# One pair of batches resident at a time, sums one slot later and deeper rings in a Mamba scan

## The chip, the cores and the metric

The kernel runs on one core of one Trainium2 chip. A core has five engines that work side by side, each through its own instructions in its own order: TensorE (PE, matrix products), VectorE (DVE), ScalarE (ACT, functions such as exp), GpSimd (POOL, slow elementwise work) and SyncE (SP, which here issues all the DMA transfers). SBUF is the memory that the engines work in, PSUM the one that PE writes to [...]. The metric is the device time of one run in microseconds; less is better. Three runs of the kernel before took 9922.25 to 9954.8 us, with a median of 9931.66 us.

## The reference

Four blocks run one after the other on images `x` of 4 batches, 96 channels and 64 x 64 places, read as sequences of L = 4096: a Mamba block with fusion (L0), a second kind of Mamba block over four scan directions (L1), a Mamba block with fusion again (L2), and a ConvNeXt block (L3). The change is in L0 and L2, which are alike:

```python
seq = x.reshape(b, c, L).transpose(0, 2, 1)
for i in range(2):
    seq = seq + _mamba_block(seq, ...)          # below
gp  = relu(x.mean((2, 3)) @ gp_w.T + gp_b)      # from the block's input
out = einsum('oc,bchw->bohw', fus_w, concat([seq as image, gp everywhere])) + fus_b
out = batchnorm(out) + x

# _mamba_block: 192 inner channels d, 16 states s
h = layernorm(seq); xs, z = split(h @ in_w)
xc = silu(conv4(xs) + conv_b)
dt, Bm, Cm = split(xc @ xproj_w)
delta = softplus(dt @ dt_w + dt_b)
dA  = exp(delta[..., None] * A)                 # per place, channel and state
dBx = delta[..., None] * Bm * xc[..., None]
hstates[l] = dA[l] * hstates[l - 1] + dBx[l]    # along the sequence
y = (sum over s of hstates * Cm) + Dp * xc
return (y * silu(z)) @ out_w
```

All numbers are 32-bit floats. The state along the sequence is what makes this expensive: 192 channels x 16 states per batch and place.

## The kernel before

The four stages follow each other in `program`: `mamba_fusion`, `ssd`, `mamba_fusion`, `convnext`. Only `mamba_fusion` changes, which runs twice.

**How its work is cut.** Batches go in pairs, and sequences in 8 chunks of T = 512. A step is (pair, layer `sub`, chunk): 2 x 2 x 8 = 32 steps a stage. The 2 x 192 inner channels of a pair fill three tiles of 128 partitions, numbered j. Inside a step the 16 states and 8 channels at a time make the 128 partitions of a scan. A group (GS = 2) is two such scans, so a step has 24 groups: j (3) x q (4) x half (2). A stage has 32 x 24 = 768 groups.

**One group** goes through these methods of `Scan`:

- `load`: DMA of the step sizes delta from a DRAM copy, each row spread over 16 partitions, into a tile `da` of 128 x 1024. For every fourth group (`dma`) a second tile `du` of the same ring is loaded, with delta times xc. The ring has 6 tiles.
- `spread`: PE makes `bs`, delta times xc spread over states, by a matmul with a selection matrix (L313), into one of two PSUM tiles of two banks. For a `dma` group, ACT writes the exponentials there instead, and POOL multiplies `du` by B (L308).
- `decay`: ACT makes the exponentials dA in place in `da` (L107).
- `scan`: DVE multiplies `bs` by B (L335; not in a `dma` group), then scans twice (L340) into `hs`; POOL multiplies `hs` by C into `hc` (L342); ACT keeps the last column in `carry` (L345). `hs` and `hc` are rings of 3.
- `sums`: PE adds the 16 states of `hc` into a PSUM tile `py` (L361), one per j and step; the term Dp * xc is a matmul into the same tile (L355).
- `close`, after the last group of a j: DVE multiplies `py` by silu(z) (L369). `project`: PE applies out_w (L377), DVE adds the result to `X` (L381). `fuse`, in the second layer alone: PE applies fus_w, ACT adds the bias, DVE takes statistics, and SyncE stores to DRAM (L507 to L513).

**What sets the order.** `Scan.run` walks over slots n. In slot n it calls `close` for group n-3, then `load` for n+4, `spread` for n+1, `decay` for n+2, `scan` for n and `sums` for n-2, then `project` for n-4 and `fuse` for n-5, and at last one or two pieces of `mamba_front` of the next step (`PACE`), so that layer norm, the input products (`pu`, `pz`), xproj (`pd`), softplus (`pt`, `delta`, `lg`) and the stores of delta are spread over the step. The framework that builds the program puts in the semaphores, gives a ring's tile again only when all that used it have finished, and may shift an instruction against the others on its engine; on the chip each engine takes its instructions in the resulting order. A wait at the head of an engine's queue so holds all that is behind it there.

**X.** `X` holds the sequence of all four batches in SBUF (96 x 4 x 4096) for the whole stage. It is loaded at the stage's start, layer 0 updates it, layer 1 updates it again, and `fuse` replaces each chunk by the fused output. During the first front DVE takes the sum of each batch (L532, `gsum`) for the global branch `gp`.

Of the kernel before, what the change touches and what calls it, by code (L numbers as in the profile page):

```python
# [18 lines left out]
F32 = mybir.dt.float32  # L19
AF = mybir.ActivationFunctionType  # L20
ALU = mybir.AluOpType
AX = mybir.AxisListType
# [132 lines left out]
def mamba_front(tc, k, X, pools, wt, pair, c, h, made):  # L155
# [14 lines left out]
    for b in range(2):  # L170
        pc = bank("pc")[:C]
        nc.tensor.matmul(
            pc, lhsT=k.center, rhs=X[:, 2 * pair + b, ds(c * T, T)], start=True, stop=True
        )
        sq = work.tile([P, T], F32, tag="ua", name="sq")[:C]
        nc.scalar.activation(sq, pc, AF.Square)
        yield
        pv = bank("pv")[:C]
        nc.tensor.matmul(pv, lhsT=k.mean, rhs=sq, start=True, stop=True)
        rs = work.tile([P, T], F32, tag="lg", name="rs")[:C]  # L180
        rsqrt(k.act, rs, pv, k.eps[:C])
        yield
        dst = h[:C, b, 3 : 3 + T]
        nc.vector.tensor_tensor(dst, pc, rs, ALU.mult)
        nc.gpsimd.tensor_scalar(dst, dst, wt["ln"][:, 0:1], wt["ln"][:, 1:2], ALU.mult, ALU.add)
# [88 lines left out]
class Scan:  # L274
# [13 lines left out]
    def load(self, g):  # L288

        for name, which in (("da", "dd"), ("du", "dg")) if g["dma"] else (("da", "dd"),):  # L290
            g[name] = self.state.tile([P, GS, T], F32, tag="da", name=name, bufs=6)
            for i in range(GS):
                r = QUART * g["quarters"][i] + HEIGHT * g["q"]
                src = g["made"][which, g["j"]][r : r + HEIGHT].partition_broadcast(NST)
                self.tc.nc.sync.dma_start(g[name][:, i], src)
# [34 lines left out]
    def scan(self, g):  # L330
        nc = self.tc.nc
        c, j = g["c"], g["j"]
        da, dbx = g["terms"]
        if not g["dma"]:
            nc.vector.tensor_tensor(dbx, dbx, self.b_or_c(g, 0), ALU.mult)  # L335
        hs = self.state.tile([P, GS, T], F32, name="hs", bufs=3)
        for i in range(GS):
            n = NQU * g["quarters"][i] + g["q"]
            init = 0.0 if c == 0 else self.carry[:, j, n : n + 1]
            nc.vector.tensor_tensor_scan(hs[:, i], da[:, i], dbx[:, i], init, ALU.mult, ALU.add)  # L340
        g["hc"] = self.state.tile([P, GS, T], F32, name="hc", bufs=3)
        nc.gpsimd.tensor_tensor(g["hc"], hs, self.b_or_c(g, 1), ALU.mult)  # L342
        if c < NT - 1:
            n = NQU * g["quarters"][0] + g["q"]
            nc.scalar.copy(self.carry[:, j, n : n + 2 * NQU + 1 : 2 * NQU], hs[:, :, T - 1])  # L345
# [25 lines left out]
    def project(self, g, b):  # L371

        nc = self.tc.nc
        xz, wt = g["made"]["xz"], g["wt"]
        po = self.psum.tile([P, T], F32, tag="po", name="po", bufs=1)[:C]
        for n, (j, r0, r1) in enumerate(ROWS[b]):
            nc.tensor.matmul(  # L377
                po, lhsT=wt["out"][r0:r1, j], rhs=xz[r0:r1, j], start=(n == 0), stop=(n == 1)
            )
        xs = self.X[:, 2 * g["pair"] + b, ds(g["c"] * T, T)]  # L380
        nc.vector.tensor_tensor(xs, xs, po, ALU.add)  # L381

    def run(self, steps, wts, front, first):
# [10 lines left out]
        ]  # L394
        total, each = len(groups), len(units)
        ahead = iter(())
        for n in range(-4, total + 6):
            slot = (n + LEAD) % each
            if slot == 0:
                for _ in ahead:  # L400
# [4 lines left out]
            def at(lag):  # L405
                return groups[n - lag] if 0 <= n - lag < total else None

            if (g := at(3)) and g["last"]:
                self.close(g)
            for stage, lag in (  # L410
                (self.load, -4), (self.spread, -1), (self.decay, -2), (self.scan, 0), (self.sums, 2),
            ):
                if g := at(lag):
                    stage(g)

            for lag, what in ((4, self.project), (5, self.fuse)):
                if (g := at(lag)) and g["last"] and g["j"] and (g["sub"] or lag == 4):
                    what(g, g["j"] - 1)
            for _ in range(PACE[slot] if slot < len(PACE) else 0):
                next(ahead, None)  # L420
# [46 lines left out]
def mamba_fusion(ctx: ExitStack, tc, k, src, dst, w):  # L467

    nc = tc.nc
    one = ctx.enter_context(tc.tile_pool(name="m1", bufs=1))  # L470
    X = one.tile([C, B, L], F32, name="X")
    for b in range(2):
        nc.sync.dma_start(X[:, b, :T], src[b, :, :T])
    work = ctx.enter_context(tc.tile_pool(name="mwork", bufs=1))
# [29 lines left out]
    stats = one.tile([C, B * NT, nc.vector.BN_STATS_DIM], F32, name="stats")  # L504

    def fuse(g, b):
        b, c = 2 * g["pair"] + b, g["c"]  # L507
        xs = X[:, b, ds(c * T, T)]
        pf = psum.tile([P, T], F32, tag="po", name="pf", bufs=1)[:C]
        nc.tensor.matmul(pf, lhsT=fus[:, 0], rhs=xs, start=True, stop=True)  # L510
        nc.scalar.activation(xs, pf, AF.Identity, bias=gb[:, b : b + 1])
        nc.vector.bn_stats(stats[:, b * NT + c], xs)
        nc.sync.dma_start(dst[b, :, ds(c * T, T)], xs)  # L513

    wts = [mamba_weights(nc, k.act, k.ident, one, w, 0, one7)]
    carry = one.tile([P, 3, P // HEIGHT], F32, name="carry")
# [3 lines left out]
        pair, sub, c = steps[n]  # L520
        return mamba_front(tc, k, X, (work, psum, dram), wts[sub], pair, c, h, made)

    for b in range(B):
        rest = slice(T if b < 2 else 0, L)
        nc.sync.dma_start(X[:, b, rest], src[b, :, rest])

    gsum = one.tile([C, B], F32, name="gsum")
    made = {}
    for n, _ in enumerate(front(0, made)):
        if n % 4 == 3 and n // 4 - 1 in range(B):  # L530
            b = n // 4 - 1
            nc.vector.reduce_sum(gsum[:, b : b + 1], X[:, b], axis=AX.X)  # L532
    wts.append(mamba_weights(nc, k.act, k.ident, one, w, 1, one7))

    gpw = one.tile([C, C], F32, name="gpw")
# [776 lines left out]
```

## Time and profile before

| stage | about, us | what runs |
|---|---|---|
| first Mamba | 0 to 3,080 | first scan 76.6, last scan ends 3,053 |
| L1 | 3,100 to 6,190 | |
| second Mamba | 6,190 to 9,250 | first scan 6,269, last scan ends 9,234 |
| ConvNeXt | 9,250 to 9,939 | |

| engine | busy, us | share of the span |
|---|---|---|
| PE | 8555.7 | 86% |
| DVE | 8200.3 | 83% |
| POOL | 6968.8 | 70% |
| ACT | 5528.2 | 56% |

| group of instructions | times | mean, ns |
|---|---|---|
| L342 POOL hc | 1536 | 2356 |
| L340 DVE scan, with carry, of da | 2016 | 1265 |
| L335 DVE bs times B | 1152 | 1214 |
| L308 POOL du times B | 384 | 2356 |

A group's line in the profile gives line, engine, operation, tiles written and read, shapes, and then busy time, the mean of one, and the idle time of the engine just before them with what ended it. A line of waits reads: engine, tile and line that waited, what it waited for, total us, times and the longest. A line of busy times by stretch gives from:to, length, then busy us and count for PE, PEld (weight loads), DVE, ACT and POOL, then the granted PE clock as a share of full speed, the DMA engines' busy share, and GB/s. A timeline's line gives start, length, engine, line and operation, and in brackets the idle time before it and who ended it. An end of a matmul is modelled, not measured.

### The profile page before, as it was taken

The numbers are of one execution on the slowest core, as the hardware profiler recorded it, in microseconds if no ns is written. First come the engines' busy times: TensorE is split into PE (matmuls) and PEld (weight loads), VectorE is DVE, ScalarE is ACT, GpSimd is POOL, SyncE is SP. The second block draws the span as 40 slices with busy tenths as digits, with TensorE's granted clock in tenths as the row PEclk, the third lists the DMA queues.
The fourth block names the chain that finished last, engine by engine and source line by source line (L and its number), as shares of the span: only waits on it lengthen the run. The fifth ranks groups of instructions, "written<-read, shape, count | busy, mean of one in ns | idle before, by whom it ended". The sixth has DMA issues, their size and how long they took to land. (4 is left out here: it accounts for less than half of the span.)

```text
span 9939.0 us, 109693 instructions
## 1 busy us (share of the span) xinstructions
PE 8555.7 (86%) x32744; PEld 3519.5 (35%) x32744; DVE 8200.3 (83%) x10861; ACT 5528.2 (56%) x10500; POOL 6968.8 (70%) x4600
## 2 busy tenths in 40 slices
PE   7888888888886998998998988788888888888688
PEld 1222212222212676776776776122222222211122
DVE  7999999999995666666666666799999999999787
ACT  5666666566663455555455554566666665665244
POOL 6888888888884555555555555688888888888322
PEclk8999999999997999999999998899999999999798
DMA  7677677677674223222222222767777777776432
GB/s 189 199 204 202 201 207 206 196 205 208 198 206 121 66 71 92 72 69 83 79 74 74 82 67 57 194 199 205 211 204 206 206 203 200 208 203 199 113 97 74
DMA packets 803535, 1528.27 MB, mean 154 GB/s; under 512 B 124253, under 2 KB 128249, under 8 KB 802170
## 3 DMA queue, kind: packets, MB, share of 16 engines
q1 hardware_dynamic: 802938, 1521.25, 54.4%
q8 instruction: 260, 4.26, 0.2%
q14 instruction: 337, 2.76, 0.1%
HBM read 1229.69 MB, written 156.37 MB: 139 GB/s over the span
## 5 line engine op out<-in xcount | busy, mean ns | idle before, releaser
L342 POOL TENSOR_TENSOR hc<-hs,bc 128x1024 f32<-128x1024 f32 x1536 | 3608.0, 2356 | 630.3 <-DVE hs L340 550.9
L340 DVE TENSOR_TENSOR_SCAN hs<-da,carry,bs 128x512 f32<-128x512 f32 x2016 | 2467.0, 1265 | 81.1 <-DVE bs L335 2.7
L107 ACT ACTIVATE da<-da,w_a 128x512 f32<-128x512 f32 x2304 | 1617.2, 716 | 1273.2 <-DMA da<-dd 1229.1
L361 PE MATMUL py<-hc,selsum 128*32 128x512 f32 x6144 | 1797.4, 637 | 469.8 <-POOL hc L342 463.4
L313 PE MATMUL bs<-du,seldu 64*128 64x512 f32 x4608 | 1570.6, 676 | 208.8 <-DVE hs L340 193.0
L335 DVE TENSOR_TENSOR bs<-bs,bc 128x1024 f32<-128x1024 f32 x1152 | 1398.4, 1214 | 180.2 <-PE bs L313 177.3
L308 POOL TENSOR_TENSOR du<-du,bc 128x1024 f32<-128x1024 f32 x384 | 904.7, 2356 | 279.8 <-DMA du<-dg 144.0
L361 PEld LDWEIGHTS py<-hc,selsum 128*32 128x32 f32 x6144 | 239.3, 110 | 1814.3 <-POOL hc L342 1125.4
L879 POOL TENSOR_TENSOR seg<-seg,cb 128x384 f32<-128x384 f32 x512 | 514.8, 1007 | 516.9 <-DVE cb L878 434.0
L863 DVE TENSOR_SCALAR seg<-dr,dac 128x128 f32<-128x128 f32 x1536 | 645.6, 454 | 276.3 <-PE y L908 269.1
L313 PEld LDWEIGHTS bs<-du,seldu 64*128 64x128 f32 x4608 | 445.6, 195 | 1202.6 <-DVE hs L340 857.0
L194 PE MATMUL pu<-h,w_conv 96*128 96x512 f32 (+3 forms) x2048 | 835.3, 628 | 11.7 <-ACT rs L107 11.6
L340 DVE TENSOR_TENSOR_SCAN hs<-bs,carry,du 128x512 f32<-128x512 f32 x672 | 823.6, 1260 | 6.7 <-issue 5.1
L814 PE MATMUL front<-pk,sconv 128*128 128x512 f32 x1536 | 756.7, 610 | 24.5 <-ACT z L802 20.4
L918 POOL TENSOR_TENSOR y<-y,xs 128x192 f32<-128x192 f32 x496 | 294.4, 594 | 626.0 <-DVE y L917 619.7
L931 ACT ACTIVATE y<-yz 128x192 f32<-128x192 f32 x512 | 186.1, 364 | 903.5 <-DVE yz L930 902.5
L883 POOL TENSOR_TENSOR xs<-pre,coef 128x576 f32<-128x576 f32 x512 | 597.1, 1171 | 65.6 <-ACT pre L112 32.4
L825 PE MATMUL front<-sconv,pk 128*128 128x192 f32 x3072 | 572.8, 329 | 51.1 <-DVE pre L830 46.0
L1175 DVE SCALAR_TENSOR_TENSOR acc<-pad,c_conv,acc 96x1024 f32<-96x1024 f32 x336 | 491.8, 1467 | 110.5 <-ACT acc L1166 59.2
L345 ACT COPY carry<-hs 128x2 f32<-128x2 f32 x1344 | 250.7, 187 | 569.7 <-DVE hs L340 566.1
L825 PEld LDWEIGHTS front<-sconv,pk 128*128 128x128 f32 x3072 | 496.5, 190 | 81.8 <-DVE pre L830 72.3
L107 ACT ACTIVATE bs<-da,w_a 128x512 f32<-128x512 f32 x768 | 522.0, 680 | 2.2 <-DMA da<-dd 0.7
(196 smaller groups left out, 13878.7 us busy)
## 6 DMA issues: line engine op xcount, KB each, us to landing
da<-dd SPq DMA_DIRECT2D x3072, 256.0 KB
du<-dg SPq DMA_DIRECT2D x768, 256.0 KB
dr<-rows SPq DMA_DIRECT2D x256, 384.0 KB
bc<-rows SPq DMA_DIRECT2D x256, 256.0 KB
dd<-delta SPq DMA_DIRECT2D x192, 256.0 KB
dg<-du SPq DMA_DIRECT2D x192, 256.0 KB
pk<-xn SPq DMA_DIRECT2D x128, 384.0 KB
pk<-xn SPq DMA_DIRECT2D x128, 256.0 KB
```

The costliest lines, as they stand in the source:

```text
L107: self.last = self.scalar.activation(out, in_, func, **kw)
L194: nc.tensor.matmul(pu[r0:r1], lhsT=wt["conv"][:kk, tap, d0:d1], rhs=h[:kk, b, ds(tap, T)], start=(tap == 0), stop=(tap == 3),)
L308: nc.gpsimd.tensor_tensor(g["du"], g["du"], self.b_or_c(g, 0), ALU.mult)
L313: nc.tensor.matmul(g["bs"][:, i], lhsT=self.sel["du"][rows, g["half"], g["q"]], rhs=g["made"]["du"][rows, g["j"]], start=True, stop=True,)
L335: nc.vector.tensor_tensor(dbx, dbx, self.b_or_c(g, 0), ALU.mult)
L340: nc.vector.tensor_tensor_scan(hs[:, i], da[:, i], dbx[:, i], init, ALU.mult, ALU.add)
L342: nc.gpsimd.tensor_tensor(g["hc"], hs, self.b_or_c(g, 1), ALU.mult)
L361: nc.tensor.matmul(py[rows], lhsT=self.sel["sum"][:, g["q"]], rhs=g["hc"][:, i], start=(g["q"] == 0), stop=(g["q"] == NQU - 1),)
L814: nc.tensor.matmul(p, lhsT=self.conv[:, i, DI + q * DST : DI + (q + 1) * DST], rhs=pk[:, i, ds(c * T, T)], start=(i == 0), stop=(i == 2),)
L825: nc.tensor.matmul(p, lhsT=pk[:, i, ds(c * Q, Q)], rhs=self.conv[:, i, :DI], start=(i == 0), stop=(i == 2),)
L863: nc.vector.tensor_scalar(seg[:, h], g["pair"]["dr"][:, c % 2 * NH + h], made["dac"][:, n0 + h : n0 + h + 1], 0.0, ALU.subtract, ALU.min,)
L883: nc.gpsimd.tensor_tensor(xs, x.to_broadcast([P, 3, NH, HD]), coef.to_broadcast([P, 3, NH, HD]), ALU.mult)
```

## The change

It has three parts.

1. `X` holds one pair of batches (96 x 2 x 4096), half of the SBUF. The second pair's sequences come in chunk by chunk: after `fuse` has stored a chunk of the first pair's output, SyncE loads the second pair's chunk into the same place. The sums for the global branch of batches 2 and 3 are taken ahead from 1024-column pieces that are loaded into tiles of the `da` ring during the first front.
2. `sums` works on group n-3 rather than n-2, and what follows it (`close`, `project`, `fuse`) moves by a slot too.
3. The rings grow with the memory that became free: `da` (step sizes) from 6 to 8 with `load` five slots ahead rather than four, `hs` (states) and `hc` (products) from 3 to 4.

It is meant to give POOL's product a slot more before PE needs it, and the loads more time ahead of their use.

```diff
-            pc, lhsT=k.center, rhs=X[:, 2 * pair + b, ds(c * T, T)], start=True, stop=True
+            pc, lhsT=k.center, rhs=X[:, b, ds(c * T, T)], start=True, stop=True
...
-            g[name] = self.state.tile([P, GS, T], F32, tag="da", name=name, bufs=6)
+            g[name] = self.state.tile([P, GS, T], F32, tag="da", name=name, bufs=8)
...
-        hs = self.state.tile([P, GS, T], F32, name="hs", bufs=3)
+        hs = self.state.tile([P, GS, T], F32, name="hs", bufs=4)
...
-        g["hc"] = self.state.tile([P, GS, T], F32, name="hc", bufs=3)
+        g["hc"] = self.state.tile([P, GS, T], F32, name="hc", bufs=4)
...
-        for n in range(-4, total + 6):
+        for n in range(-5, total + 7):
...
-            if (g := at(3)) and g["last"]:
+            if (g := at(4)) and g["last"]:
                 self.close(g)
             for stage, lag in (
-                (self.load, -4), (self.spread, -1), (self.decay, -2), (self.scan, 0), (self.sums, 2),
+                (self.load, -5), (self.spread, -1), (self.decay, -2), (self.scan, 0), (self.sums, 3),
             ):
...
-            for lag, what in ((4, self.project), (5, self.fuse)):
-                if (g := at(lag)) and g["last"] and g["j"] and (g["sub"] or lag == 4):
+            for lag, what in ((5, self.project), (6, self.fuse)):
+                if (g := at(lag)) and g["last"] and g["j"] and (g["sub"] or lag == 5):
                     what(g, g["j"] - 1)
...
-    X = one.tile([C, B, L], F32, name="X")
+    X = one.tile([C, 2, L], F32, name="X")
...
-        nc.sync.dma_start(dst[b, :, ds(c * T, T)], xs)
+        nc.sync.dma_start(dst[n, :, t], xs)
+        if g["pair"] == 0:
+            nc.sync.dma_start(xs, src[2 + b, :, t])
...
+        if n in (13, 15, 17, 19):
+            for m in range(n - 13, n - 11):
+                b, c = 2 + m // (L // BLK), m % (L // BLK)
+                x = state.tile([P, GS, T], F32, tag="da", name="x", bufs=8)[:C]
+                nc.sync.dma_start(
+                    x, src[b, :, ds(c * BLK, BLK)].rearrange("c (i t) -> c i t", i=GS)
+                )
+                nc.vector.reduce_sum(parts[:, b, c : c + 1], x.rearrange("c i t -> c (i t)"), axis=AX.X)
+    nc.vector.reduce_sum(gsum[:, 2:], parts[:, 2:], axis=AX.X)
```

## The prediction

> **What bounds the kernel now.** I read the page's share per engine and its 40 slices first, then busy time by stage, then the waits of each engine in a scan stage, then the timeline of one step. The two Mamba stages are alike, some 3,000 us each; VectorE (DVE) is the busiest engine in both:
>
> ```profile
> 200.00:1000.00 800.00, 701.36 (x2126) 162.34 (x2124) 743.61 (x688) 498.95 (x892) 682.01 (x328) 0.95 0.71 202
> 1000.00:2000.00 1000.00, 877.35 (x2690) 203.03 (x2686) 932.86 (x862) 618.83 (x1114) 849.62 (x408) 0.95 0.72 203
> 7000.00:8000.00 1000.00, 866.89 (x2712) 202.20 (x2712) 941.70 (x877) 630.71 (x1131) 860.58 (x414) 0.97 0.73 206
> ```
>
> The columns are PE, PEld, DVE, ACT, POOL, clock, DMA. DVE works 93 to 94% of the time, PE 87%, POOL 85%. No edit takes an instruction off DVE inside the scans, so the gain can only come out of the 6 to 7% in which DVE is idle. Its waits in 200 to 3,000 us (total, times, longest):
>
> ```profile
> DVE bs L335 <- PE bs L313: 85.5, 73, 4.2
> DVE lg L270 <- ACT pt L268: 17.6, 30, 2.7
> DVE h L184 <- ACT rs L107: 15.4, 19, 1.9
> DVE X L381 <- PE bs L313: 12.9, 5, 2.8
> DVE xz L369 <- PE py L361: 6.8, 4, 3.4
> ```
>
> In 6,200 to 9,200 us the same five are 86.0, 18.8, 30.7, 7.8 and 8.7 (and 2.5 for X behind po). So over both stages: for bs 171.5 us, lg 36.4, h 46.1, X 23.2, xz 15.5; together 293 us. The rest of DVE's idle time is gaps of some 0.1 us between a product and its scan, which nothing here touches. 293 us is the whole purse. The largest entry is DVE waiting for PE to make bs. PE, in turn, waits for POOL:
>
> ```profile
> PE py L361 <- POOL hc L342: 207.6, 249, 4.2
> PE bs L313 <- DVE hs L340: 87.1, 138, 1.6
> PE pc L172 <- DVE lg L270: 39.4, 26, 3.4
> ```
>
> The second is harmless (PE is early, the buffer is still being scanned). The first is PE standing before the sums (L361) of a group whose product hc POOL hasn't finished. How that reaches DVE shows in one step, PE's timeline and then DVE's:
>
> ```profile
> 1425.20 1.05 PE L361 MATMUL py<-hc,selsum 128*32 128x512 f32 x4 [0.66 <-POOL hc L342]
> ...
> 1427.61 1.05 PE L361 MATMUL py<-hc,selsum 128*32 128x512 f32 x4 [0.35 <-POOL hc L342]
> ...
> 1431.32 1.05 PE L361 MATMUL py<-hc,selsum 128*32 128x512 f32 x4 [0.56 <-POOL hc L342]
> 1432.30 1.13 PE L204 MATMUL pz<-h,w_in 96*128 96x512 f32 x2
> 1433.36 2.08 PE L217 MATMUL pd<-xz,w_xproj 128*64 128x512 f32 x8
> 1435.37 1.13 PE L313 MATMUL bs<-du,seldu 64*128 64x512 f32 x4
> ```
>
> ```profile
> 1432.32 2.45 DVE L340 TENSOR_TENSOR_SCAN hs<-da,carry,bs 128x512 f32<-128x512 f32 x2
> 1436.55 1.23 DVE L335 TENSOR_TENSOR bs<-bs,bc 128x1024 f32<-128x1024 f32 x1 [1.78 <-PE bs L313]
> ```
>
> PE lost 0.66 + 0.35 + 0.56 = 1.57 us on hc, then did two pieces of the next step's front (pz, pd), and came to bs too late: DVE stood for 1.78 us. From 1,000 to 1,500 us (5.4 steps of 93 us) DVE's gaps of over 0.6 us before L335 are 1.18, 1.78, 1.68, 1.33, 0.70, 1.32, 0.81, 1.41 and 1.78, 12.0 us, or 2.2 us a step.
>
> **What the Trainium skill says.** "Perfetto Trace Analysis", Optimization Strategy: a gap that recurs on the engine that should be saturated can mean too few buffers; the 2.2 us a step agree in that they recur, though what is short here is the distance of the sums more than buffers. "TensorE: Matmul & The Clock Gate", The mechanism: matmuls start and end strictly in order; so do they above, with pz, pd and bs behind a waiting py. The same page, What's actually happening: after an idle window of some 3.4 us PE's clock falls to half. The trace agrees: its stretches at half clock last 3.4, 6.8, 10.2 or 17.1 us. One of them (granted clock is the third column from the right; PE had just stood 1.7 us for lg):
>
> ```profile
> 880.00:895.00 15.00, 11.13 (x32) 2.63 (x32) 13.28 (x15) 10.54 (x19) 13.31 (x7) 1.00 0.91 259
> 895.40:912.50 17.10, 16.57 (x22) 3.51 (x22) 12.90 (x14) 7.89 (x16) 15.54 (x10) 0.50 0.68 199
> ```
>
> "DMA: Bandwidth & Descriptors", Anatomy of one DMA: a DMA's semaphore wait is spent on the issuing sequencer. SyncE's queue shows it: `SPq L245 <- DMA rows<-dbl` is 104.0 us in 30 waits, 3.5 us each, until a store has landed.
>
> **The change, part by part.**
>
> *Sums a slot later (lag 2 to 3; close, project and fuse follow).* In slot n PE makes bs(n+1), free once scan(n-1) has ended, and then the sums of n-2. A slot is 2,800 us / 724 groups = 3.87 us. POOL can start hc(n-2) when scan(n-2) ends and needs 2.36 us (L342: mean 2356 ns). PE comes to the sums about 3.87 + 1.13 = 5.0 us after that end, so a POOL that is 2.6 us late stops PE; one product du (L308, also 2.36 us) in front of it nearly suffices, two of the front's small products are 2.5 us. One slot more lifts this to 6.5 us. The longest wait before was 4.2 us and would be gone, but for 0.3 us. So the 207.6 us (some 420 over both stages) of PE's waits fall to about none. They are not DVE's time: most lie beside scans that run meanwhile. What passes to DVE is part of the purse:
> - bs, 171.5 us. At the recurring gap 1.57 of 1.78 us is hc, 88%. At other places PE is late through its own front work, or at half clock, or behind pc waiting for lg (39.4 us in this stage, untouched). Ends: 0 and 88%, 151 us. I take 60%: 103 us.
> - h, 46.1 us: h needs rs, rs needs PE's pv, which stands behind the sums in its slot. Some 12 us of it are the first step. I take 40%: 18 us (ends 0 and 34).
> - X, 23.2 us: project's matmul stands right behind the sums. Half: 12 us (0 to 23).
> - lg, 36.4 us: DVE, ACT and DVE again in turn (delta, pt, lg); nothing of this is changed: 0. xz, 15.5: mostly the last step, which drains: 0.
>
> Sum 103 + 18 + 12 = 133 us. Drain: one slot more at the end of each stage has no new work in it: 0.
>
> *Rings hs and hc 3 to 4.* hc needs the fourth because its reader is a slot later; POOL waits for PE's py 26.2 us in this stage, and this stays or falls. hs: DVE doesn't wait for POOL beyond 0.5 us: 0.
>
> *Ring da 6 to 8, loads at lag -5.* Four groups take five tiles (every fourth loads du too). Six tiles are 4.8 groups: the load for n+4 waits for scan n-0.8 and ACT uses it in slot n+2, 2.8 slots or 10.8 us after. Eight tiles are 6.4 groups: the load for n+5 waits for scan n-1.4, use in slot n+3, 4.4 slots or 17 us. ACT's waits for da (560.9 us, 346 times, 1.6 us each) should mostly go, but ACT is 62% busy and DVE waits for its exponentials 1.0 us: 0 on the path. It helps POOL's du, which waits 67.6 us for its load: that is in the hc lag already.
>
> *One pair of X.* Sixteen reloads a stage on SyncE, each after fuse's store has landed: 3.5 us each, 56 a stage, with loads queued behind. The added 6.2 us of lead cover one such stop: 0; if none were covered, 112 us over both. 3.1 MB more a stage are 15 us of DMA at 203 GB/s, beside 3,000 us in which DMA is 72% busy: 0. Reduces: two of 4.42 us (4096 columns) become eight of 1024, some 1.2 us by size, in the prologue where DVE mostly waits; the first scan waits for weights that SyncE issues until 72.6 us: 0, at most 5 us a stage either way.
>
> *A step's xz buffer* (two) is given free by project, now a slot later, in the slot in which ACT first writes the next one. ACT may stand for 1 to 2 us a step, with bs and da exponentials behind it; DVE is a slot away: 0.
>
> Time: 9,932 - 133 = 9,799; I say **9,800**.
>
> **The rivals.**
> - *Nothing moves* (9,920): PE at bs stays behind its own 3.2 us of pz and pd, DVE waits as before. For: a fifth or so of the bs waits lies near half clock, and PE is 87% busy. Against: 1.57 of 1.78 us above. Within 0.3%.
> - *More than I take* (9,690): half-clock stretches begin mostly within 2 us of PE standing for hc or for lg (at 605.3, 861.3 and 1072.9 us for hc, 1.4 to 2.1 us each); without the first kind, fewer begin, and PE meets nearly every bs. 151 + 34 + 23 plus most of lg, some 240 us off. Against: pc waiting for lg up to 3.4 us begins stretches too, and remains.
> - *Slower* (10,045): reloads hold SyncE and the loads behind come late, 112 us; or the shifted project and fuse and the front fall so on PE's queue that a second gap of 1.8 us a step appears, 64 x 1.8 = 115 us. For: the order of instructions on an engine isn't the program's (pt among bs at 1,436 us), so it may shift. Against: lead of 17 us, and PE has 13% idle.
>
> **How the numbers follow.** Forecast 0.57 (between 9,740 and 9,890), more 0.15, nothing 0.13, slower 0.15. All of the removable terms give 9,690, none of them 9,932. Of the case "more" about half lies below 9,690, of the slower one about two thirds above 9,945, some 0.18 together; so the range is 9,690 to 9,945. Faster by over 0.3% (below 9,902): 0.57 + 0.15 = 0.72. Same 0.13, slower 0.15.
>
> **What would show it.** Right: PE's wait of py for hc near zero, bs on DVE at some 35 us a stage, DVE at 95 to 96% in 1,000 to 2,000 us, a step of 91 us, ACT's wait for da a third or less. Wrong: bs still 85 us a stage with hc gone (PE's own work), or DVE waiting for ACT da or POOL du (SyncE held up), or more half-clock time.

## The result and the profile after

The changed kernel is slower: 9977.1 us in the median of four runs (9974.94 to 9984.03) against 9926.95 for the kernel before, a ratio of 1.0047 with a 95% interval of 1.0030 to 1.0064. 9,800 was forecast. (In the changed kernel's numbering `load` to `project` keep their lines; `fuse` is L511 to L516, the reload L516.)

Busy time by stage, columns as in the prediction. DVE, which was to rise to 95 or 96%, fell from 93.3 and 94.2 to 92.8 and 92.0%, and PE's clock is lower in the second Mamba stage:

```profile
1000.00:2000.00 1000.00, 868.04 (x2668) 203.66 (x2666) 928.03 (x861) 610.64 (x1098) 845.37 (x407) 0.95 0.76 205
7000.00:8000.00 1000.00, 865.49 (x2636) 204.16 (x2636) 920.01 (x855) 601.36 (x1084) 838.71 (x405) 0.94 0.76 204
```

What DVE waited for in 200 to 3,000 us (total, times, longest):

```profile
DVE bs L335 <- PE bs L313: 120.4, 69, 5.8
DVE delta L267 <- ACT lg L107: 15.5, 26, 1.4
DVE h L184 <- ACT rs L107: 6.7, 13, 1.2
DVE stats L513 <- ACT X L512: 5.9, 5, 1.4
DVE xz L369 <- PE py L361: 4.6, 1, 4.6
DVE X L381 <- PE po L377: 4.1, 3, 1.4
```

The wait of lg for pt (17.6 us before) is gone from the list, h and X are halved or better; delta's wait for lg rose from 3.5 to 15.5, and one for fuse's statistics is new. But the wait for bs, the heart of the forecast, rose from 85.5 to 120.4 us, and from 86.0 to 134.1 in the second stage. The waits for bs, delta, lg, h, X, xz and stats in both stages add up to 306 us before and 356 after; the kernel became 50 us longer. And PE's wait for hc, which was to vanish, is there in fewer and longer pieces (113 of 1.7 us for 249 of 0.8):

```profile
PE py L361 <- POOL hc L342: 188.5, 113, 4.6
PE bs L313 <- DVE hs L340: 135.5, 139, 2.8
```

The place that the prediction took apart, the spread of group 15 (groups of a step are numbered 0 to 23), is as it was. PE's timeline of a step of the first layer, then DVE's:

```profile
503.22 1.05 PE L361 MATMUL py<-hc,selsum 128*32 128x512 f32 x4 [1.39 <-POOL hc L342]
504.20 1.13 PE L204 MATMUL pz<-h,w_in 96*128 96x512 f32 x2
505.26 2.08 PE L217 MATMUL pd<-xz,w_xproj 128*64 128x512 f32 x8
507.27 1.13 PE L313 MATMUL bs<-du,seldu 64*128 64x512 f32 x4
```

```profile
504.22 2.45 DVE L340 TENSOR_TENSOR_SCAN hs<-da,carry,bs 128x512 f32<-128x512 f32 x2
508.45 1.23 DVE L335 TENSOR_TENSOR bs<-bs,bc 128x1024 f32<-128x1024 f32 x1 [1.78 <-PE bs L313]
```

The sums in front of pz are those of group 12 in both kernels (counted along PE's instructions), though the program issues them a slot later now. The 1.78 us are those of the step that the prediction showed; the mean over 20 steps of the first layer is 1.75 us before and 1.76 after.

A second gap has come, at the spread of group 22. PE:

```profile
528.93 1.92 PE L361 MATMUL py<-hc,selsum 128*32 128x512 f32 x4 [3.65 <-POOL hc L342]
530.78 2.02 PE L377 MATMUL po<-xz,w_out 64*96 64x512 f32 x2
532.73 2.02 PE L172 MATMUL pc<-X,center 96*96 96x512 f32 x2
534.68 1.92 PE L361 MATMUL py<-hc,selsum 128*32 128x512 f32 x4
536.54 1.58 PE L313 MATMUL bs<-du,seldu 64*128 64x512 f32 x4
```

PE stands 3.65 us for hc of group 18, then runs the next instructions at half clock (sums 1.92 us where 1.05 is normal), and DVE waits 2.05 us at 538.17 (2.1 in the mean of 20 steps). Why hc 18 is late is seen on POOL:

```profile
521.63 2.36 POOL L308 TENSOR_TENSOR du<-du,bc 128x1024 f32<-128x1024 f32 x1 [0.18 <-DMA du<-dg]
523.96 1.27 POOL L271 TENSOR_TENSOR delta<-delta,lg 128x512 f32<-128x512 f32 x1
525.30 1.27 POOL L248 TENSOR_TENSOR du<-delta,xz 128x512 f32<-128x512 f32 x1
526.53 2.35 POOL L342 TENSOR_TENSOR hc<-hs,bc 128x1024 f32<-128x1024 f32 x1
```

The product of the loaded du (of group 21) stands ahead of hc 18. In the kernel before it came after it; the pair of hc here is groups 17 and 18:

```profile
517.35 4.67 POOL L342 TENSOR_TENSOR hc<-hs,bc 128x1024 f32<-128x1024 f32 x2
522.29 2.35 POOL L308 TENSOR_TENSOR du<-du,bc 128x1024 f32<-128x1024 f32 x1 [0.26 <-issue]
524.60 2.35 POOL L342 TENSOR_TENSOR hc<-hs,bc 128x1024 f32<-128x1024 f32 x1
```

Counted along POOL's instructions, five of a step's six du products stand a group earlier than before; with the loads put back (an experiment below) all six are where they were. The page's groups show the deeper ring doing what it was made for: ACT stands 769 us for its loads instead of 1,273 and POOL's du product 57 instead of 280. Before:

```profile
L107 ACT ACTIVATE da<-da,w_a 128x512 f32<-128x512 f32 x2304 | 1617.2, 716 | 1273.2 <-DMA da<-dd 1229.1
L308 POOL TENSOR_TENSOR du<-du,bc 128x1024 f32<-128x1024 f32 x384 | 904.7, 2356 | 279.8 <-DMA du<-dg 144.0
```

After:

```profile
L107 ACT ACTIVATE da<-da,w_a 128x512 f32<-128x512 f32 x2304 | 1607.7, 716 | 768.9 <-DMA da<-dd 744.1
L308 POOL TENSOR_TENSOR du<-du,bc 128x1024 f32<-128x1024 f32 x384 | 905.1, 2357 | 56.8 <-DMA du<-dg 49.3
```

**Where the time is lost.** The mean length of a step, from its first scan to the next one's, over both stages, worked out from the scans' starts in the trace (us; "change" are the steps next to a change of layer or pair, numbers 7 to 9, 15 to 17, 23 to 25 of 0 to 31; first layer 2 to 6 and 18 to 22, second 10 to 14 and 27 to 29). Kernels are described below:

| kernel | first layer | second layer | change | ratio to before, 95% |
|---|---|---|---|---|
| before | 92.4 | 93.0 | 92.0 | |
| changed | 92.1 | 92.5 | 95.4 | 1.0047 (1.0030 to 1.0064) |
| loads and ring da put back | 92.5 | 92.9 | 92.3 | 0.9996 (0.9987 to 1.0005) |
| X alone | 92.7 | 93.8 | 92.4 | 1.0031 (1.0021 to 1.0041) |
| sums a slot later alone | 92.7 | 92.8 | 92.8 | 1.0017 (1.0009 to 1.0025) |
| changed, sums put back | 92.5 | 96.7 | 94.4 | 1.0104 (1.0074 to 1.0134) |
| changed, all sums held | 90.0 | 94.8 | 92.7 | 0.9986 (0.9974 to 0.9997) |
| all sums held, loads put back | 93.6 | 95.0 | 93.7 | 1.0086 (1.0072 to 1.0100) |
| changed, du product held | 91.2 | 92.4 | 96.1 | 1.0051 (1.0039 to 1.0063) |
| changed, sums held in layer 0 | 90.3 | 92.7 | 93.9 | 0.9983 (0.9975 to 0.9991) |
| the same, and at changes | 90.0 | 93.1 | 91.9 | 0.9940 (0.9922 to 0.9958) |

The regular steps of the changed kernel are even a little shorter than before. The loss is 3.4 us in each of 18 steps at a change, 61 us, which outweighs 0.3 x 20 + 0.5 x 16 = 14 us won; the scans' spans of the two stages together are 43.5 us longer. DVE's waits of over 0.3 us tell the same: in a step at a change they are 4.3 us in the kernel before and 7.8 in the changed one. Of the 3.5 us more, 2.9 are waits for bs, most of them at groups 2, 17, 22 and 23.

### The profile page after: what moved, and what is told of

It reads as the page before. It is cut to its first block, busy times and chain, and to the rows that moved or that the text cites. A ratio compares the mean times of both kernels' runs of the same rounds, so it can differ in the third digit from the quotient of the medians.

```text
span 9973.8 us, 108964 instructions
## 1 busy us (share of the span) xinstructions
PE 8589.1 (86%) x32744; PEld 3527.1 (35%) x32744; DVE 8201.1 (82%) x10875; ACT 5513.8 (55%) x10450; POOL 6955.9 (70%) x4600
## 5 line engine op out<-in xcount | busy, mean ns | idle before, releaser
L361 PE MATMUL py<-hc,selsum 128*32 128x512 f32 x6144 | 1774.9, 651 | 437.0 <-POOL hc L342 409.0
L313 PE MATMUL bs<-du,seldu 64*128 64x512 f32 x4608 | 1511.4, 676 | 297.4 <-DVE hs L340 289.5
```

The costliest lines, as they stand in the source:

```text
L313: nc.tensor.matmul(g["bs"][:, i], lhsT=self.sel["du"][rows, g["half"], g["q"]], rhs=g["made"]["du"][rows, g["j"]], start=True, stop=True,)
L361: nc.tensor.matmul(py[rows], lhsT=self.sel["sum"][:, g["q"]], rhs=g["hc"][:, i], start=(g["q"] == 0), stop=(g["q"] == NQU - 1),)
```

## The experiments

### Parts undone or done alone

Sums back to lag 2, all else as changed:

```diff
-            if (g := at(4)) and g["last"]:
+            if (g := at(3)) and g["last"]:
...
-                (self.load, -5), (self.spread, -1), (self.decay, -2), (self.scan, 0), (self.sums, 3),
+                (self.load, -5), (self.spread, -1), (self.decay, -2), (self.scan, 0), (self.sums, 2),
...
-            for lag, what in ((5, self.project), (6, self.fuse)):
+            for lag, what in ((4, self.project), (5, self.fuse)):
```

> The changed kernel with sums, close, project and fuse a slot earlier again (lags 2, 3, 4, 5); rings of 8, 4 and 4, loads five ahead and one pair of X stay. If the loss lies in the earlier loads, which let POOL take the product du in front of hc of group 18, PE's stand of some 3.4 us there and DVE's gap of 2.4 us before bs of group 22 stay: 9,960 to 9,990 us. If the loss lies in the shifted sums and project, it is gone: 9,930 or less.

10047.1 us, ratio 1.0104 (1.0074 to 1.0134), beyond both expectations. PE's stand for hc 18 stayed, some 100 us a stage; the second layer's steps grew most (96.7 us).

Loads and their ring back:

```diff
-            g[name] = self.state.tile([P, GS, T], F32, tag="da", name=name, bufs=8)
+            g[name] = self.state.tile([P, GS, T], F32, tag="da", name=name, bufs=6)
...
-                (self.load, -5), (self.spread, -1), (self.decay, -2), (self.scan, 0), (self.sums, 3),
+                (self.load, -4), (self.spread, -1), (self.decay, -2), (self.scan, 0), (self.sums, 3),
```

> The changed kernel with the da ring at 6 and loads four ahead again; sums a slot later, hs and hc rings of 4 and one pair of X stay. If the earlier loads make the stand at hc of group 18, it goes and with it up to 64 gaps of 2.4 us: 9,830 to 9,900 us. If they don't, 9,960 to 9,990.

9940.69 us, 0.9996 (0.9987 to 1.0005), between the two expectations: the loss is gone, and no gain came in its place.

Only X of one pair, with its reloads and reduces, in the kernel before:

> Of the change only one pair of X at a time: lags, rings and loads are those of the kernel before. If the reloads hold SyncE's queue, or the steps at a change of layer or pair grow by 4 to 9 us through X, 9,960 us or more. If X costs nothing, 9,915 to 9,940, as before.

9973.09 us, 1.0031 (1.0021 to 1.0041): X costs something, as the first of the two expectations had it.

Only the sums later (close, project and fuse with them), with all of X:

```diff
-        g["hc"] = self.state.tile([P, GS, T], F32, name="hc", bufs=3)
+        g["hc"] = self.state.tile([P, GS, T], F32, name="hc", bufs=4)
...
-                (self.load, -4), (self.spread, -1), (self.decay, -2), (self.scan, 0), (self.sums, 2),
+                (self.load, -4), (self.spread, -1), (self.decay, -2), (self.scan, 0), (self.sums, 3),
```

> The kernel before with all of X and loads as before, only the sums one slot later and the ring of hc at four (hs stays at three, for room). Theory (the parts add up: 0.9996 with X of one pair, which alone costs 0.31 %): ratio 0.996 to 0.997, some 9900 us. Rival (the later sums only repair what X of one pair costs): 0.999 to 1.001. If the prediction's full sum held, the gain would be 1.3 %: 0.987.

9946.19 us, 1.0017 (1.0009 to 1.0025); both expectations missed.

So the parts don't add up. The later sums alone cost 0.17%; on top of X of one pair, and with hs and hc in rings of four, they bring 0.35% (1.0031 to 0.9996), on top of the deep loads 0.57% (1.0104 to 1.0047). Nothing of it is near the 1.3% forecast. The deep loads, costed at nothing, cost 0.51% (0.9996 to 1.0047). X, costed at nothing, costs 0.31%. Is that the reloads?

```diff
-        if g["pair"] == 0:
-            nc.sync.dma_start(xs, src[2 + b, :, t])
```

> The kernel before with X of one pair and nothing else of the change, and without the eight reloads in the loop: the second pair then starts from the fused output of the first, not from its own input, which leaves the work of every instruction the same. Theory (X costs 0.3 % through the reloads, which stop SyncE or come among the loads): ratio to the kernel before 0.999 to 1.001. Rival (it costs through the prologue and the order that the planner makes of the rest): it stays at 1.003.

9953.35 us, 1.0021 (1.0009 to 1.0033), between the two expectations; the interval overlaps that with the reloads. SyncE's stop before the reload is small in the changed kernel (`SPq L516 <- DMA raw<-X` 18.2 us in 8 waits). The order of the instructions isn't it either: without the reloads, PE, DVE, ACT, POOL and SyncE take theirs from the first scan on in the order of the kernel before, but for three pairs of neighbouring matmuls, and in these single profiles the scans of the second stage still take 21 us longer, those of the first 3 us less. Where X's 0.31% lies stays open.

### The sums held behind the spreads

If the order on PE's queue undid the later slot, an order edge (no semaphore, only a rule for the compile-time order) should bring the gain back:

```diff
-            nc.tensor.matmul(                 # spread, L313
+            self.last_bs = nc.tensor.matmul(
...
-            nc.tensor.matmul(                 # sums, L361
+            ins = nc.tensor.matmul(
+            self.k.act._behind(ins, self.last_bs)
```

> The changed kernel with one thing added: on PE the sums of a group are kept behind the bs matmuls that the program lists ahead of them, so that they stand three to four groups behind bs in the whole step rather than in its first ten groups only. If the loss comes from sums that stand one or two groups behind bs in the second half, PE's waits for hc fall from 188 us to under 60 in 200 to 3,000 us and the gaps before bs of groups 15 and 22 shrink: 9,830 to 9,900 us. If PE is late by its own work, the waits for hc fall and the time stays at 9,960 to 9,990.

9928.41 us, 0.9986 (0.9974 to 0.9997): 0.6% better than the changed kernel. At group 15, PE:

```profile
495.04 1.13 PE L313 MATMUL bs<-du,seldu 64*128 64x512 f32 x4
496.10 1.05 PE L361 MATMUL py<-hc,selsum 128*32 128x512 f32 x4
```

and DVE:

```profile
496.22 1.23 DVE L335 TENSOR_TENSOR bs<-bs,bc 128x1024 f32<-128x1024 f32 x1 [0.31 <-PE bs L313]
497.58 2.45 DVE L340 TENSOR_TENSOR_SCAN hs<-da,carry,bs 128x512 f32<-128x512 f32 x2
```

1.78 us have become 0.31. PE's wait for hc, 188.5 us in the changed kernel, has left the list of waits, and the step of the first layer is 2.4 us shorter than in the kernel before, about what was forecast (133 us over 64 steps are 2.1). The second layer's is 2.3 us longer than in the changed kernel. DVE's waits in 200 to 3,000 us:

```profile
DVE delta L267 <- ACT lg L107: 63.3, 55, 2.4
DVE bs L335 <- PE bs L313: 49.5, 54, 3.2
DVE stats L514 <- ACT X L513: 13.5, 14, 2.4
```

Now delta waits for lg (15.5 us before the edge), and DVE's statistics for fuse's X. delta's wait is 2.0 us a step in either layer. In the first it is outweighed, as the waits for bs fall from 3.9 to 0.3 us; in the second they stay near 2.9, now at groups 2 and 3. A likely reason for delta's wait is that pt stands on PE behind held sums: in the step shown its last matmul ends 6.0 us after the spread of group 15 begins, in the changed kernel 3.9. That was not tried by itself.

The same edge with the loads put back:

> The changed kernel with both corrections: ring of step sizes back to 6 and loads back to four slots ahead, and every sums matmul kept behind the spread matmuls issued before it. Theory (the two losses, early order of the sums and deep loads, add up): the gain of the order, 0.6 % with deep loads, comes on top of the 0.9996 of the loads put back alone, so the ratio to the kernel before is 0.993 to 0.996, some 9880 to 9900 us, and the steps at a change of layer stay near 92 us. Rival (order and shallow loads are two cures of one loss, since both take the stand of PE at group 18 away): nothing is added, ratio 0.998 to 1.000.

10014.69 us, 1.0086 (1.0072 to 1.0100). Both expectations failed, by their sign. The wait for bs is down here too, to 60.1 us in 200 to 3,000, but lg waits 57.4 us for pt, delta 41.6 for lg, and h 16.0. So the deep loads, and the early du product with them, are not only harm: with the sums held, the kernel is 1.0% better with deep loads than without.

### The du product held behind hc

```diff
-            nc.gpsimd.tensor_tensor(g["du"], g["du"], self.b_or_c(g, 0), ALU.mult)
+            ins = nc.gpsimd.tensor_tensor(g["du"], g["du"], self.b_or_c(g, 0), ALU.mult)
+            if len(self.hcs) > 1:
+                self.k.act._behind(ins, self.hcs[-2])
```

> The changed kernel with one ordering edge on POOL: each product of a loaded du with B is kept behind the product hc of three groups before it, as it lay in the kernel before; loads stay five slots ahead. Theory (the deep loads cost because their early data let the compile-time order put the du product of group 21 ahead of hc 18, and PE stands 3.6 us for it): PE's wait for hc at group 18 falls from 95 us a stage to under 30, the half clock stretch at group 19 goes, and the time falls to that of the loads put back, ratio to the kernel before 0.999 to 1.000. Rival (the deep loads cost through the transfers themselves, on SyncE or the queues): the ratio stays at 1.004, with the wait at group 18 gone or not.

9978.6 us, 1.0051 (1.0039 to 1.0063), no better than the changed kernel. The wait at group 18 fell as the theory asked, from 94.2 to 28.5 us a stage; but in a regular step of the first layer the stand of 3.64 us broke up into 1.13, 1.04 and 1.80 us at groups 18 to 20, and PE's wait for hc in all stayed (181.3 us for 188.5 in 200 to 3,000). A regular step of the first layer gained 0.9 us (92.1 to 91.2). The steps at a change were 96.1 us, and they decide. This isn't quite the order of the kernel before, though: counted along POOL's instructions, there only the product of group 21 stood right behind the hc of three groups before it, the other five of a step one group earlier; the edge puts all six there. So the theory (this one product explains the loss) found no support in the time, and an edge on group 21 alone was not tried.

### Spare matmuls against the half clock

The changed kernel has 833 us at half clock between the first and last scans of its two stages, the one before 577 (the expectations below use other counts, 700, 614 and 680; the table has one count for all). A spare matmul reads states that a scan has left in `hs` and writes a PSUM tile that nobody reads; order edges, not shown, keep it in its place:

```diff
+            dm = self.psum.tile([P, T], F32, tag="po", name="dm", bufs=1)
+            nc.tensor.matmul(dm, lhsT=self.k.ident, rhs=g["hs"][:, 0], start=True, stop=True)
```

> The changed kernel with three spare matmuls a step on TensorE, whose result nobody reads: two between the spread of group 22 and the sums of group 18, where TensorE stands 3.5 us a step, and one ahead of the spread of group 4, where it stands 2.0. They read the states of the scan before, so they run inside the stand (1.05 us each, estimated from a full 128x512 pair of passes). Theory (the stands themselves cost nothing; the clock, halved in the 3.4 us window after one with TensorE busy less than about half, makes the spreads late): half clock goes at groups 2 and 19, the regular step falls from 92.1 to 90 or 90.5 us, ratio to the kernel before 0.990 to 0.997. Rival (the half clock falls where nothing depends on it, and the order of the queues sets the step): the regular step stays at 92 or more, ratio 1.003 to 1.008.

> The same with the du product held behind hc, where the half clock had moved from group 19 to group 23: one spare matmul each ahead of the sums of groups 18 to 21 and of the spread of group 4. Clock theory: the half clock of 614 us in the two stages falls under 200, regular steps from 91.2 to 90 us, ratio 0.990 to 0.997. Rival: no better than without them, 1.004 to 1.008.

> The kernel before with four spare matmuls a step, one each ahead of the sums of groups 15, 16, 19 and 20, where its TensorE stands for hc (and has 700 us of half clock in the two stages). Clock theory: half clock under 350 us, mean step from 92.4 to 91 us or less, ratio 0.985 to 0.993. Rival: 1.000 to 1.004, as the four matmuls only push the spreads back.

> The kernel before with the sums one slot later and hc in a ring of four, as in the earlier run with only that, and five spare matmuls a step, ahead of the sums of groups 12, 15, 16, 19 and 20. Clock theory: half clock from 680 us to under 350, ratio 0.985 to 0.993. Rival: 1.001 to 1.005.

| base | half clock, us | first layer | second | change | ratio to before |
|---|---|---|---|---|---|
| changed | 833 to 441 | 92.0 | 94.9 | 94.3 | 1.0078 (1.0053 to 1.0103) |
| du product held | 625 to 301 | 91.9 | 94.0 | 93.3 | 1.0013 (1.0006 to 1.0019) |
| before | 577 to 458 | 93.6 | 95.2 | 93.3 | 1.0094 (1.0079 to 1.0108) |
| sums a slot later alone | 553 to 645 | 96.2 | 102.1 | 98.1 | 1.0377 (1.0363 to 1.0390) |

In the first two kernels the half clock was halved, and no regular step got near 90 us; the first came out as its rival said, the second between the two. In the third it fell by a fifth and in the fourth it rose, so these two don't test the theory. That the half clock costs nothing isn't shown, as the spare work takes PE's time too. But the time doesn't follow it: the fastest kernel of all, further down, has 652 us of it, more than the kernel before. The second row is the one gain (1.0051 to 1.0013), and it comes in the steps at a change, 96.1 to 93.3 us. The last row brought a wait of its own: `DVE xz` for `PE py` 92.8 us, and scans waiting for hc 27.3 us in 200 to 3,000 us, where hs has a ring of three.

What the half clock does at a change is seen at the start of step 9 of the changed kernel. PE:

```profile
919.99 1.92 PE L361 MATMUL py<-hc,selsum 128*32 128x512 f32 x4 [1.78 <-POOL hc L342]
921.84 1.75 PE L179 MATMUL pv<-sq,mean 96*96 96x512 f32 x2
923.53 1.12 PE L313 MATMUL bs<-du,seldu 64*128 64x512 f32 x2
924.58 1.12 PE L194 MATMUL pu<-h,w_conv 96*128 96x512 f32 x2
925.64 1.12 PE L313 MATMUL bs<-du,seldu 64*128 64x512 f32 x2
```

DVE:

```profile
925.01 0.69 DVE L184 TENSOR_TENSOR h<-pc,rs 96x512 f32<-96x512 f32 x1 [1.17 <-ACT rs L107]
926.80 1.23 DVE L335 TENSOR_TENSOR bs<-bs,bc 128x1024 f32<-128x1024 f32 x1 [1.09 <-PE bs L313]
```

The last sums of step 8 stand for a late hc. They and most of pv behind them run at half clock, 1.92 and 1.75 us where 1.05 and 1.10 are normal, some 1.5 us in all. Then the order adds its part, at full clock again: the next spread comes in two halves with pu between, and takes 3.2 us from its start to its end where a spread takes 1.13. h and bs wait in turn, 2.3 us together in this profile.

### One edge at the one place

If the wait for the spread of group 15 is time that can be had by itself, moving only what is in front of it should bring 90 to 100 us.

```diff
+            if (g["j"], g["q"], g["half"]) == (1, 2, 0):     # sums of group 12
+                self.k.act._behind(ins, self.bs15)           # spread of group 15
```

> The kernel before with one order edge a step: the sums of group 12 behind the spread of group 15, nothing else. Theory of the one place: the wait for that spread goes from 1.78 us to about 0.3 in each step, as where all sums were held, 1.45 x 62 = 90 us, ratio 0.990 to 0.993. Rival (the wait comes back elsewhere in the step): 0.998 to 1.002.

> The changed kernel with the same single edge. Theory of the one place: 90 us less than the changed kernel, ratio to the kernel before 0.995 to 0.997, regular steps 90.6 us. Rival: 1.003 to 1.006.

and pd instead, one slot later by `PACE` and behind the spread:

```diff
-PACE = (1,) * 8 + (2,) + (1,) * 7 + (2,) + (1,) * 7
+PACE = (1,) * 8 + (2,) + (1,) * 9 + (2,) + (1,) * 5
...
+            k.act._behind(ins, k.act.last_bs)                # pd, L217
```

> The kernel before with the front's projection pd one slot later and behind the spread issued before it, so that the spread of group 15 no longer stands behind its four matmuls (2.0 us). Theory of the one place: the wait of 1.78 us goes to zero, 103 us less, ratio 0.988 to 0.992. Rival: pd, delta and du come 1 to 2 us later and the wait comes back at the steps of the front (delta, lg), 0.998 to 1.003.

> The kernel before with both edits: sums of group 12 and pd behind the spread of group 15. Theory of the one place: no more than either alone, as one wait can go only once, 0.988 to 0.992. Rival: 0.998 to 1.003.

DVE's waits of over 0.3 us in a step of the first layer, mean of 20 steps, worked out from the trace (us; "all" has a tenth or so of other waits):

| kernel | bs of group 15 | other bs | delta, lg | h, X, xz | all | ratio to before |
|---|---|---|---|---|---|---|
| before | 1.8 | 0.6 | 0.5 | 1.3 | 4.3 | |
| sums of 12 held | 0.1 | 2.1 | 2.5 | 1.0 | 5.8 | 1.0047 (1.0032 to 1.0062) |
| pd held | 0.0 | 2.9 | 0.6 | 1.7 | 5.3 | 1.0109 (1.0094 to 1.0123) |
| both | 0.0 | 2.1 | 1.0 | 1.4 | 4.5 | 1.0043 (1.0028 to 1.0058) |
| changed | 1.8 | 2.1 | 0.6 | 0.0 | 4.5 | 1.0047 (1.0030 to 1.0064) |
| changed, sums of 12 held | 0.0 | 2.1 | 1.6 | 0.3 | 4.1 | 1.0009 (1.0001 to 1.0018) |
| changed, all sums held | 0.3 | 0.0 | 2.0 | 0.2 | 2.6 | 0.9986 (0.9974 to 0.9997) |

The wait at group 15 goes every time, and comes back at other instructions of the same step, as the rivals said. Their numbers missed: on the kernel before all three edits cost more than the rivals allowed (1.0043 to 1.0109). In the changed kernel the edge brought 0.4% (1.0047 to 1.0009), less than half of the 90 us, and not in regular steps (91.9 and 92.8 us, 92.1 and 92.5 without it) but at the changes, 93.5 us for 95.4. How the wait comes back is seen in the kernel before with the one edge. PE has the spread in time:

```profile
504.89 1.13 PE L314 MATMUL bs<-du,seldu 64*128 64x512 f32 x4
505.95 1.05 PE L364 MATMUL py<-hc,selsum 128*32 128x512 f32 x4
506.94 0.69 PE L235 MATMUL pt<-dbl,w_dt 64*128 64x512 f32 x1
```

and DVE:

```profile
506.07 1.23 DVE L338 TENSOR_TENSOR bs<-bs,bc 128x1024 f32<-128x1024 f32 x1 [0.16 <-PE bs L314]
507.44 2.45 DVE L343 TENSOR_TENSOR_SCAN hs<-da,carry,bs 128x512 f32<-128x512 f32 x2
509.80 1.21 DVE L338 TENSOR_TENSOR bs<-bs,bc 128x1024 f32<-128x1024 f32 x1
513.45 0.69 DVE L267 SCALAR_TENSOR_TENSOR delta<-pt,lg 128x512 f32<-128x512 f32 x1 [2.44 <-ACT lg L107]
514.06 2.44 DVE L343 TENSOR_TENSOR_SCAN hs<-da,carry,bs 128x512 f32<-128x512 f32 x2
```

DVE is 1.6 us further at group 15, then meets delta, an instruction of the next step's front, in front of a scan that has its data. lg is not there (ACT has exponentials for the scans in front of it, the last of them over at 512.9), and DVE stands 2.44 us.

### A version that beats both

The edge on all sums, only in the steps where it paid:

```diff
+            if not g["sub"]:                                       # first layer
+                self.k.act._behind(ins, self.last_bs)
```

> The changed kernel with every sums matmul held behind the spreads issued before it, but only in the steps of the first layer. Theory (a step's gain and loss belong to the order in that step): steps of the first layer 90 us, of the second 92.5, ratio to the kernel before 0.992 to 0.997. Rival (an order in one layer's steps sets off waits in the next ones): 0.998 to 1.003.

9917.41 us, 0.9983 (0.9975 to 0.9991). Regular steps are as expected (90.3 and 92.7 us), but those at a change take 93.9, and the ratio is in the rival's range. And with the first two and the last chunk of the second layer:

```diff
+            if not g["sub"] or g["c"] in (0, 1, NT - 1):
```

> The same, held also in the first two and the last chunk of the second layer, where the changed kernel loses 3 to 4 us a step against before and the fully held one does not. Theory: 18 us better than the last run, ratio 0.990 to 0.996. Rival: 0.998 to 1.003.

9872.76 us, 0.9940 (0.9922 to 0.9958), 1.1% less than the changed kernel by the ratios (0.9940 / 1.0047); 45 us better than the last run, where 18 were expected. Steps take 90.0, 93.1 and 91.9 us. Its waits and busy time:

```profile
DVE bs L335 <- PE bs L313: 52.3, 49, 3.1
DVE delta L267 <- ACT lg L107: 45.4, 47, 2.3
```

```profile
1000.00:2000.00 1000.00, 863.22 (x2714) 202.94 (x2712) 945.17 (x878) 626.33 (x1126) 858.39 (x414) 0.95 0.78 209
7000.00:8000.00 1000.00, 863.18 (x2696) 202.97 (x2692) 939.99 (x875) 620.37 (x1118) 856.34 (x414) 0.95 0.78 209
```

DVE is back at 94 to 94.5%, and bs at 52 us where the prediction looked for some 35.

## Why the prediction was wrong, point by point

- **"So the 207.6 us of PE's waits fall to about none": the step that failed.** It put PE's queue in the order of the program's slots, by which the latest spread ahead of a group's sums is three groups on before and four after. Worked out along PE's instructions, it was 2 to 3 before and 3 to 4 after in groups 0 to 9, but mostly 1 to 3 in both kernels from group 10 on, where nine tenths of the waits lie. So the slot gave POOL nothing there, and hc kept 188.5 of 207.6 us. With an order edge on the sums these waits went. The trace of before had the order already, and the prediction's own rival had seen that it isn't the program's. Why the compile-time order put the sums there is not shown.
- **bs, 103 us of the sum.** Over both stages bs stands at 254.5 us for 171.5. With the order held the wait at group 15 did go (1.78 to 0.31), and bs fell to 93.6, 78 of the 103 us; so this mechanism was right and its condition missing. That kernel is 12 us faster than the one before.
- **The purse of 293 us as a sum of separate waits.** This failed too, and no single size would mend it. A wait that goes lets DVE run into the next instruction that isn't ready: 4.3 us a step became 5.8, 5.3 or 4.5 when the largest entry of 1.8 was taken away alone. Even with the sums held and hc waited for no more, the purse of both stages, delta and stats counted in, went only from 306 to 290 us: bs lost 78, and delta's wait for lg rose from 11 to 137. "lg, nothing of this is changed: 0" was the weak point, as delta, of the same chain, takes up what the others leave. The purse itself was the right place to look: from the 306 us of the kernel before it went to 356 in the changed one, 290 with all sums held and 255 in the last version, changes of +50, -16 and -51 where the times changed by +50, -12 and -59.
- **h 18 and X 12 us.** Over both stages h went from 46.1 to 26.9 and X from 23.2 to 10.1, 19 and 13 us less. These came, at the sizes given, and were eaten by bs. That PE's shorter waits brought them, as the prediction had it, was not tried.
- **Ring da, "0 on the path".** The waits it was to shorten did shorten (ACT for da 560.9 to 333.2 us, not to the third expected). But with the deeper loads the compile-time order has their consumer ahead of hc 18. On the path the deep loads are 0.51%, for the most part at changes of layer and pair (95.4 us a step for 92.3 with the loads put back).
- **One pair of X, 0.** Measured +0.31%; the stop of SyncE, which was named as the danger, is 18 us in the first stage, and leaving the reloads out changed little (1.0031 to 1.0021). The cause of the 0.31% stays open.
- **The rival "slower"** (chance 0.15) said that the shifted instructions might fall so that a second gap of 1.8 us a step appears. It did, at group 22 with 2.05 us; in regular steps of the first layer the gains on h and X pay for most of it (waits of 4.3 us before, 4.5 after), and at a change they don't. Its reason, a shifted order on PE's queue, came true on POOL's; its 10,045 us was too much, as it took all 64 steps without such gains.

Open: what in the deep loads lengthens the steps at a change. These take 94.4 to 96.1 us in the three kernels with loads at -5 and free sums (changed, sums put back, du product held). With the sums of group 12 alone held they take 93.5, with all sums held there 91.9 to 92.7; in the kernel before, and with X or the later sums alone, 92.0 to 92.8. But the deep loads are not the only way to such steps: with loads at -4, they take 94.4 to 94.6 us where pd was moved, and 93.7 where all sums were held. As most of these edits shift other instructions too, a ratio here is that of a whole order, not the price of one edge.

## What to carry to other kernels

Before a lag in the source is costed, look at the trace for where the instruction really sits on its engine's queue: if the order is made at compile time, a later slot in the source need not move it, and an order edge may be what is wanted. Don't add up the waits of an engine that runs in order as if each could be cashed in alone: ask of each, what the engine meets next if this one is gone, and whether that is ready. A buffer that brings data earlier can go with a loss, and the early work may be put in front of something more urgent; take parts apart and measure them, since here their effects even changed sign with each other. And an edge meant to restore an order should be compared with the order that was there.

## What the runs showed of the hardware

PE's clock fell to half after far less than an empty window. In the changed kernel's two scan stages, with every stretch at full clock cut into windows of 3.41 us, all 97 windows in which PE was busy less than 47% were the last ones before a half-clock stretch; of 1,285 windows with more than 67%, none; in between 25 of 123. In the kernel before it was 55 of 57, 4 of 1,312 and 31 of 198 (PE's busy time is modelled, so the edges are rough). So a stand of 1.8 us in the right place is enough: in step 9 above PE was busy 1.71 of the 3.41 us ahead of the half clock. The Trainium skill, "TensorE: Matmul & The Clock Gate", What's actually happening, gives one idle window as the condition; here a window about half idle was enough. Its window length agrees: 169 of the changed kernel's 188 half-clock stretches last 3.4, 6.8 or 10.2 us.

The regular step of the changed kernel's first layer, 92.1 us, is 27 such windows (27 x 3.413 = 92.2), and its half-clock stretches came at the same two groups in step after step. Whether the step locks to the windows was not tried; the 90.0 us of the kernels with the sums held, 26.4 windows, show that it need not have such a length.
